# Running sums and maxima in a mixture-of-experts router: a chain of small additions, or one masked product and one reduction

## The chip, the core and the metric

The kernel runs on one core of one Trainium2 chip. The metric is device time in microseconds (us) of one execution; before the change the median of three runs is 1411.22 us (1411.13 to 1414.11). A profile is one execution recorded by the hardware profiler. Its times are counted from the start of its span, and all places in time below are such times.

## What is computed

A decoder layer over 16 sequences of 100 tokens (1600 tokens, width 512): self-attention, cross-attention over 361 context positions, and a feed-forward part with 8 experts, each part followed by a residual sum and a layer norm. The change touches the feed-forward part's routing:

```python
logits = jnp.einsum('bsd,de->bse', x, router_w) + router_b
topk_vals, topk_idx = jax.lax.top_k(logits, TOP_K)          # TOP_K = 2 of E = 8
topk_w = jax.nn.softmax(topk_vals, axis=-1)
full_w = jnp.sum(jax.nn.one_hot(topk_idx, E, dtype=x.dtype) * topk_w[..., None], axis=-2)
h = jnp.einsum('td,edf->etf', xf, expert_w) + expert_b[:, None, :]
combined = jnp.einsum('etf,te->tf', jax.nn.silu(h), full_w.reshape(-1, E))
out = jnp.einsum('bsd,df->bsf', combined, proj_w) + proj_b
y = x + out
return norm_w * (y / jnp.sqrt(jnp.mean(y * y, axis=-1, keepdims=True) + EPS))
```

## The kernel before

**Tiles.** The 1600 tokens are 13 tiles (`NT`) of 128 tokens, the last one of 64. Each token is sent to two experts. The kernel sorts the 3200 (token, expert) pairs into 32 slots (`NSL`) of 128 rows, each slot belonging to one expert, so that an expert product runs over 128 full rows. For each slot it gathers the rows of `x2d` by an indirect DMA on GpSimd's queue (`e_gather`, L1265), transposes them on TensorE (`e_turn`, tile `pte`, L1281), splits the transposed rows into a high and a low part (ScalarE writes the high part, L137, VectorE or GpSimd the low part, L140) and multiplies them by the expert's weights in three products (`e_product`, tile `ph`, L145 to L147, whose weights' address is read from the table `wat` by TensorE's sequencer, L1287). Every matmul of this kernel is such a triple over a high and a low part.

**Order.** Each engine runs its instructions in a fixed order, which a scheduler chose when the program was built; it may interleave the source's statements. An instruction that waits holds up everything behind it on its engine. POOL in the profile is GpSimd, DVE is VectorE, ACT is ScalarE, SP is the queue that issues most DMAs.

**Routing, in three steps.** `choose(a, b)` (L1041) takes the two best experts of the tokens in tiles a to b and counts, by two small matmuls (L1080), each token's rank within its expert; a third one (L1091) gives counts per tile. `settle(a, b)` (L1135) decides which slot each (tile, expert) opens. `slots(a, b, upto)` (L1231) turns this into lists of row indices for the slots a to b: small matmuls (L1239) of `named` (a token's number at its place in a slot, L1126) with `is_in` (the slot of a token, L1224), then the copies `idx`, `wat` and `bat` (L1247 to L1251), on which the gathers and the expert products wait.

This happens twice. The tiles 0 to 8 (`CUT` is 9) are settled while the last products of cross-attention's output projection still run (tile `acc`, L145 to L147, 128x512, four head products each of tiles 10, 11 and 12); that gives the slots 0 to 10 (`EARLY` is 11). The tiles 9 to 12 are settled while TensorE works on the early slots; that gives the slots 11 to 31.

**The code that changes.** In `settle` the helper `before_it` needs, for every tile, the number of slots opened by all earlier tiles. It keeps a running sum in `opened` (or `filled`), one VectorE addition of one element per tile:

```python
for t in range(a, b):
    nc.vector.tensor_tensor(
        till[:, t + 1 : t + 2], till[:, t : t + 1], here[:, t - a : t - a + 1], ALU.add)
```

(L1168). It runs for `opened` over 9 tiles and later 4, and for `filled` over 9. A third loop (L1207) keeps the running maximum `last`, 8 elements per tile, over 9 and later 4 tiles. `settle` then ends with `new` (L1211 to L1218), `tile_of` (L1223) and `is_in` (L1224), each twice from L1222 on.

**Around it.** While the first settle runs, VectorE also makes low parts `ot_l` of what the `acc` products read, and GpSimd makes low parts `ot_l` and `WL` (L140). `WL` belongs to expert weights, which arrive by DMA as `f_e` (L1320). The attention output arrives as `of` (L822).

Of the kernel before, what the change touches and what calls it, by code (L numbers as in the profile page):

```python
# [9 lines left out]
FP = mybir.dt.float32  # L10
FR = mybir.dt.float32r
AF = mybir.ActivationFunctionType
ALU = mybir.AluOpType
AX = mybir.AxisListType
# [13 lines left out]
NE = 8  # L28
# [34 lines left out]
def tile_decoder_layer(  # L63
# [28 lines left out]
    nc = tc.nc  # L92
# [3 lines left out]
    def pool(stack, name, bufs=1, **k):  # L96
        return stack.enter_context(
            tc.tile_pool(name=name, bufs=bufs, reuse_waits="tile", **k)
        )
# [115 lines left out]
    NT = len(TT)  # L215
# [56 lines left out]
    for k in range(KC):  # L272
# [8 lines left out]
        out=causal,  # L281
        in_=causal,
        compare_op=ALU.is_ge,
        fill=1.0e30,
        base=0,
        pattern=[[-1, S]],
        channel_multiplier=1,
# [526 lines left out]
    parts = [(t, g) for t in range(NT - TAIL) for g in range(NKV)]  # L814
# [94 lines left out]
    gw = pool(gs, "gate", side="right")  # L909
# [55 lines left out]
    I32, HF = mybir.dt.int32, mybir.dt.float16  # L965
    NSL = NE + (2 * T - NE) // 128
    CUT, EARLY = NT - 4, 11
# [3 lines left out]
    def iota(p, shape, pattern, base=0, mult=0, name=""):  # L971
# [17 lines left out]
        out=before,  # L989
        in_=before,  # L990
        compare_op=ALU.is_gt,
        fill=0.0,
        base=0,
        pattern=[[1, 128]],
        channel_multiplier=-1,
# [5 lines left out]
        out=lower,  # L1001
        in_=lower,
        compare_op=ALU.is_gt,
        fill=0.0,
        base=0,
        pattern=[[1, NE], [-1, NE]],
        channel_multiplier=0,
# [5 lines left out]
    cum = gw.tile([128, NT + 1, NE], HF, name="cum")  # L1013
    nc.vector.memset(cum[:, 0, :], 0.0)
    full = gw.tile([128, NE], FP, name="full")
    opened = gw.tile([128, NT + 1], FP, name="opened")
    nc.vector.memset(opened[:, 0:1], float(EARLY))
    filled = gw.tile([128, CUT + 1], FP, name="filled")
    nc.vector.memset(filled[:, 0:1], 0.0)
    last = gw.tile([128, NT + 1, NE], FP, name="last")  # L1020
    nc.vector.memset(last[:, 0, :], 0.0)
    rank = gw.tile([128, NT, NE], FP, name="rank")
    lo = gw.tile([128, 2, NT], FP, name="lo")
    tile_of = gw.tile([128, 2, NT], FP, name="tile_of")
# [4 lines left out]
    def by_128(dst, src, name):  # L1029

        i = gw.tile(list(dst.shape), I32, name=f"i_{name}")
        nc.vector.tensor_copy(i, src)
        nc.vector.tensor_scalar(i, i, 7, None, ALU.arith_shift_right)
        nc.vector.tensor_copy(dst, i)

    def table(name, shape, dt=FP):

        size = [128, CUT + 1, *shape[2:]]
        return gw.tile(size, dt, name=name, tag=name)[:, : shape[1]]
# [95 lines left out]
    def settle(a, b):  # L1135

        m = b - a
        sh = [128, m, NE]
        o2, o3 = 2 * NE + CUT * NE, (2 + CUT + m + 1) * NE
        count = gb[:, o2:o3].rearrange("p (b e) -> p b e", e=NE)  # L1140
        if a == 0:
            by_128(full, count[:, m, :], "full")

        up = table("up", [128, m + 1, NE])
        nc.vector.tensor_scalar(up, count, 127.0, None, ALU.add)
        had = table("had", [128, m + 1, NE])
        by_128(had, up, f"had_{a}")

        opn = table("opn", sh)
        nc.vector.tensor_tensor(opn, had[:, 1:, :], had[:, :m, :], ALU.subtract)  # L1150
        had = had[:, :m, :]
        sh4 = [128, m, NE, NE]

        def before_it(these, till, less, name):

            part = table("parts", sh4, HF)
            nc.vector.tensor_tensor(
                part,
                lower.unsqueeze(1).to_broadcast(sh4),
                these.unsqueeze(2).to_broadcast(sh4),  # L1160
                ALU.mult,
            )
            new = table(name, sh)
            nc.vector.tensor_reduce(new, part, AX.X, ALU.add)
            here = table("here", [128, m])
            nc.vector.tensor_reduce(here, these, AX.X, ALU.add)
            for t in range(a, b):
                nc.vector.tensor_tensor(  # L1168
                    till[:, t + 1 : t + 2],
                    till[:, t : t + 1],  # L1170
                    here[:, t - a : t - a + 1],
                    ALU.add,
                )
            nc.vector.scalar_tensor_tensor(
                new,
                new,
                float(less),
                till[:, a:b].unsqueeze(2).to_broadcast(sh),
                ALU.subtract,
                ALU.add,  # L1180
            )
            return new


        new = before_it(opn, opened, EARLY if a else 0, "new")
        if a == 0:
            fills = table("fills", sh)
            nc.vector.tensor_tensor(
                fills, had, full.unsqueeze(1).to_broadcast(sh), ALU.is_lt
            )  # L1190
            nc.vector.tensor_tensor(fills, fills, opn, ALU.mult)
            first = before_it(fills, filled, 0, "first")

            nc.vector.scalar_tensor_tensor(
                new, first, float(EARLY), new, ALU.min, ALU.subtract
            )

            nc.vector.scalar_tensor_tensor(
                fills, first, float(EARLY), fills, ALU.is_lt, ALU.mult
            )  # L1200
            nc.vector.tensor_tensor(first, first, new, ALU.add)
            nc.vector.tensor_tensor(first, first, fills, ALU.mult)
            nc.vector.tensor_tensor(new, first, new, ALU.subtract)

        nc.vector.tensor_tensor(opn, opn, new, ALU.mult)
        for t in range(a, b):
            nc.vector.tensor_tensor(  # L1207
                last[:, t + 1, :], last[:, t, :], opn[:, t - a, :], ALU.max
            )
        old = last[:, a:b, :]  # L1210
        nc.vector.tensor_tensor(new, new, old, ALU.subtract)  # L1211

        past = table("past", sh)
        nc.vector.scalar_tensor_tensor(
            past, had, 128.0, rank[:, a:b, :], ALU.mult, ALU.is_le
        )
        nc.vector.tensor_tensor(new, new, past, ALU.mult)
        nc.vector.tensor_tensor(new, new, old, ALU.add)  # L1218
        sh3 = [128, m, NSL]
        for j in range(2):  # L1220
            mine = table("chose", sh)
            nc.vector.tensor_tensor(mine, one[:, j, a:b, :], new, ALU.mult)  # L1222
            nc.vector.tensor_reduce(tile_of[:, j, a:b], mine, AX.X, ALU.add)  # L1223
            nc.vector.tensor_tensor(  # L1224
                is_in[:, j, a:b, :],
                seq[:, :NSL].unsqueeze(1).to_broadcast(sh3),
                tile_of[:, j, a:b].unsqueeze(2).to_broadcast(sh3),
                ALU.is_equal,
            )
# [98 lines left out]
    for i in range(HEAD * NKV, len(parts)):  # L1328
        t, g = parts[i]
# [29 lines left out]
        if (t, g) == (CUT, 3):  # L1359
            settle(0, CUT)  # L1360
            slots(0, EARLY, CUT)
# [29 lines left out]
    with tc.high_priority(offset=URGENT):  # L1391
        choose(CUT + 1, NT)
        settle(CUT, NT)
        slots(EARLY, NSL, NT)
# [412 lines left out]
```

## Time and profile before

| what | us |
|---|---|
| median of the runs | 1411.22 |
| the profiled execution, whole | 1423.84 |
| its span | 1422.1 |
| first `settle` to the end of its `is_in`, on VectorE | 1178.8 to 1212.0 |
| first lookup matmuls (L1239), TensorE | 1211.16 to 1213.2 |
| gathers of the slots 0 to 3 issued, GpSimd | 1213.90 to 1219.1 |
| second `settle` to its last `is_in` | 1252.8 to 1261.9 |
| second lookups end, TensorE | 1266.3 |
| first gather of the second list issued | 1267.17 |
| TensorE starts on the first gathered rows of the second list | 1273.74 |

The profiled execution took 12.6 us longer than the median of the runs, so differences are taken within the trace and then set against the median. In the timelines a row reads: start, duration, engine, line, operation, output<-inputs, size, count, and in square brackets how long the engine sat idle before it and what ended that. A row with a count (x7) covers that many instructions in a row. The granted clock (PEclk) is TensorE's clock as a share of full speed.

### The profile page before, as it was taken

Reading aid. Unit: us, or ns where it says so; the run is one execution under the profiler, and the core shown is the slowest. Engines: PE = TensorE matmul, PEld = TensorE weight load, DVE = VectorE, ACT = ScalarE, POOL = GpSimd, SP = SyncE. Lnnn points to the kernel's source line nnn. Section 1 sums busy time; section 2 is a strip of 40 time slices with the busy share of each in tenths; the row PEclk is TensorE's granted clock in tenths of the full one; section 3 lists DMA queues with packets and bytes.
Section 4 is the critical chain, followed back from the end, with each engine's and each line's share of the span. In section 5 each row is a group of like instructions: output and inputs, shape, how many; then the busy total and the mean of one; then the engine's idle time right before and its main releaser. Section 6 shows DMA issues by size and latency. Waiting matters only on the chain.

```text
span 1422.1 us, 25158 instructions
## 1 busy us (share of the span) xinstructions
PE 1338.8 (94%) x7952; PEld 1109.5 (78%) x7952; DVE 939.8 (66%) x2960; ACT 756.9 (53%) x1899; POOL 708.8 (50%) x837
## 2 busy tenths in 40 slices
PE   8999989999999999999999999999999897899895
PEld 6888868888878887888888788878887675677773
DVE  5776577776467777767777667767653658654577
ACT  4666653444445666666565666656563233233356
POOL 6877663344245555555555545545454345431530
PEclk9999989999999999999999999999999999799997
DMA  5221254545442222233233213232536555667773
GB/s 158 72 93 51 73 158 115 130 91 111 101 93 77 53 60 69 70 77 76 69 70 82 70 43 70 70 70 54 132 84 198 170 167 164 189 207 232 247 254 125
DMA packets 197872, 159.79 MB, mean 112 GB/s; under 512 B 133322, under 2 KB 152878, under 8 KB 197742
## 3 DMA queue, kind: packets, MB, share of 16 engines
q1 hardware_dynamic: 187904, 137.83, 36.3%
q0 software_dynamic: 4576, 14.95, 3.5%
q10 hardware_dynamic: 5262, 5.41, 1.3%
q8 instruction: 65, 1.06, 0.3%
q14 instruction: 65, 0.53, 0.1%
HBM read 107.16 MB, written 50.99 MB: 111 GB/s over the span
## 4 chain that ended last, share of the span: by engine, by line
PE 69%; DVE 13%; DMA 8%; ACT 4%; issue 3%; POOL 1%; SPq 1%; ACTq 0%; DVEq 0%; POOLq 0%
PE pq L145 4%; PE pq L147 4%; PE pq L146 4%; PE pv L145 4%; PE pv L146 4%; PE pv L147 4%; PE ptp L767 3%; PE pk L145 3%; PE pk L147 3%; PE pk L146 3%; PE s L145 3%; PE s L147 3%; PE s L146 3%; PE av L146 2%; PE av L145 2%
## 5 line engine op out<-in xcount | busy, mean ns | idle before, releaser
L759 POOL TENSOR_SCALAR p<-p,sums 100x361 f32<-100x361 f32 x256 | 146.5, 577 | 100.2 <-DVE sums L758 89.2
L746 DVE CUSTOM_DVE_ANT_0 p<-s,nmask 100x361 f32<-100x361 f32 x256 | 132.9, 527 | 64.4 <-PE s L147 56.0
L757 ACT ACTIVATE p<-p,nm 100x361 f32<-100x361 f32 x256 | 153.2, 601 | 40.1 <-DVE nm L746 37.0
L140 DVE TENSOR_TENSOR pT_l<-ptp,pT_h 128x400 fp32r<-128x400 f32 (+1 forms) x192 | 107.4, 567 | 57.3 <-ACT pT_h L137 56.7
L145 PE MATMUL pq<-WH 128*128 128x512 f32 (+2 forms) x272 | 107.2, 394 | 5.7 <-DVE WH L139 5.7
L767 PE MATMUL ptp<-ident,p 100*128 100x100 f32 (+1 forms) x768 | 107.5, 252 | 0.0
L137 ACT CAST pT_h<-ptp 128x400 fp32r<-128x400 f32 (+1 forms) x192 | 91.2, 486 | 29.6 <-PE ptp L767 29.1
L767 PEld LDWEIGHTS ptp<-ident,p 100*128 100x128 f32 (+1 forms) x768 | 95.6, 152 | 13.4 <-POOL p L759 2.3
L140 POOL TENSOR_TENSOR cT_l<-cf,cT_h 128x512 fp32r<-128x512 f32 (+1 forms) x48 | 54.3, 1133 | 101.9 <-ACT cT_h L137 100.0
L146 PE MATMUL pq<-WL,WH 128*128 128x512 f32 (+2 forms) x272 | 104.6, 385 | 0.0
L147 PE MATMUL pq<-WH,WL 128*128 128x512 f32 (+2 forms) x272 | 104.5, 384 | 0.0
L147 PE MATMUL acc<-WH,ot_l 128*128 128x512 f32 (+1 forms) x208 | 85.9, 414 | 7.4 <-DVE ot_l L140 5.6
L145 PE MATMUL acc<-WH,ot_h 128*128 128x512 f32 (+1 forms) x208 | 85.8, 413 | 4.9 <-ACT ot_h L137 4.9
L145 PE MATMUL s<-kT_h,WH 128*100 128x362 f32 x256 | 88.2, 355 | 1.7 <-ACT kT_h L137 1.7
L145 PE MATMUL av<-pT_h,WH 128*128 128x400 f32 (+1 forms) x192 | 77.3, 402 | 11.5 <-ACT pT_h L137 11.2
L147 PE MATMUL s<-kT_h,WL 128*100 128x362 f32 x256 | 84.5, 330 | 0.0
L146 PE MATMUL acc<-WL,ot_h 128*128 128x512 f32 (+1 forms) x208 | 84.3, 405 | 0.0
L146 PE MATMUL s<-kT_l,WH 128*100 128x362 f32 x256 | 83.9, 328 | 0.0
L614 POOL TENSOR_TENSOR qs<-qs,r_q 128x512 f32<-128x512 f32 (+1 forms) x52 | 54.0, 1068 | 59.3 <-DVE r_q L169 48.9
L140 POOL TENSOR_TENSOR WL<-qf,WH 128x400 fp32r<-128x400 f32 x64 | 67.3, 1052 | 30.1 <-ACT WH L137 26.7
L145 PE MATMUL pv<-WH,cT_h 128*128 128x512 f32 (+1 forms) x192 | 79.6, 414 | 0.9 <-DVE WL L140 0.9
L145 PE MATMUL pk<-WH,cT_h 128*128 128x512 f32 (+1 forms) x192 | 77.6, 404 | 0.2
(336 smaller groups left out, 4007.0 us busy)
## 6 DMA issues: line engine op xcount, KB each, us to landing
qf<-qd SPq DMA_DIRECT2D x64, 200.0 KB
of<-od SPq DMA_DIRECT2D x48, 256.0 KB
cf<-in_ctxT SPq DMA_DIRECT2D x16, 722.0 KB
eb<-in_expert_b SPq DMA_DIRECT2D x32, 256.0 KB
ysd<-h SPq DMA_DIRECT2D x32, 256.0 KB
f_e<-in_expert_w SPq DMA_DIRECT2D x30, 256.0 KB
f_wq<-in_Wq SPq DMA_DIRECT2D x16, 256.0 KB
f_wo<-in_Wo SPq DMA_DIRECT2D x16, 256.0 KB
```

The costliest lines, as they stand in the source:

```text
L137: ins = nc.scalar.copy(dst.h, src)
L140: low.tensor_tensor(dst.l, src, dst.h.bitcast(FP), ALU.subtract)
L145: nc.tensor.matmul(out, a.h, b.h, start=start, stop=False)
L146: nc.tensor.matmul(out, a.h, b.l, start=False, stop=False)
L147: nc.tensor.matmul(out, a.l, b.h, start=False, stop=stop)
L614: nc.gpsimd.tensor_tensor(qr[:, hs, :], qr[:, hs, :], rs[:n, hs].unsqueeze(2).to_broadcast([n, GR, HD2]), ALU.mult,)
L746: nc.vector.tensor_tensor_reduce(out=p, in0=sc[:, :SE], in1=nmask, scale=1.0, scalar=BIG, op0=ALU.add, op1=ALU.min, accum_out=nm,)
L757: nc.scalar.activation(p, p, AF.Exp, bias=nm, scale=-1.0, accum_out=sh)
L759: nc.gpsimd.tensor_scalar(p, p, sh, 1.0, ALU.mult, ALU.mult)
L767: nc.tensor.transpose(pt[:n, h, :], probs[h][:, c0 : c0 + n], ident[:S, :S])
```

## The change

The three loops go. A constant table `earlier` of 13 x 13 elements is made once on GpSimd (a memset and an affine select): it is 1 where the second tile number is below the first. The sum over earlier tiles is then one VectorE product of `earlier` with the per-tile values and one reduction; the maximum over earlier tiles is a product of 9 x 8 x 9 elements (later 4 x 8 x 13) and one reduction by max. The three tables that held the running values lose their start elements and the memsets of these.

```diff
+    earlier = gw.tile([128, NT, NT], FP, name="earlier")
+    nc.gpsimd.memset(earlier, 1.0)
+    nc.gpsimd.affine_select(
+        out=earlier, in_=earlier, compare_op=ALU.is_gt, fill=0.0, base=0,
+        pattern=[[1, NT], [-1, NT]], channel_multiplier=0,
+    )
...
-            here = table("here", [128, m])
-            nc.vector.tensor_reduce(here, these, AX.X, ALU.add)
-            for t in range(a, b):
-                nc.vector.tensor_tensor(
-                    till[:, t + 1 : t + 2],
-                    till[:, t : t + 1],
-                    here[:, t - a : t - a + 1],
-                    ALU.add,
-                )
+            nc.vector.tensor_reduce(here[:, a:b], these, AX.X, ALU.add)
+            tri = parts_of([128, 1, m, b])[:, 0]
+            nc.vector.tensor_tensor(
+                tri,
+                earlier[:, a:b, :b],
+                here[:, :b].unsqueeze(1).to_broadcast([128, m, b]),
+                ALU.mult,
+            )
+            till = table("till", [128, m])
+            nc.vector.tensor_reduce(till, tri, AX.X, ALU.add)
...
-        nc.vector.tensor_tensor(opn, opn, new, ALU.mult)
-        for t in range(a, b):
-            nc.vector.tensor_tensor(
-                last[:, t + 1, :], last[:, t, :], opn[:, t - a, :], ALU.max
-            )
-        old = last[:, a:b, :]
+        nc.vector.tensor_tensor(places[:, a:b, :], opn, new, ALU.mult)
+        sh5 = [128, m, NE, b]
+        prior = parts_of(sh5)
+        nc.vector.tensor_tensor(
+            prior,
+            places[:, :b, :].rearrange("p t e -> p e t").unsqueeze(1).to_broadcast(sh5),
+            earlier[:, a:b, :b].unsqueeze(2).to_broadcast(sh5),
+            ALU.mult,
+        )
+        old = table("old", sh)
+        nc.vector.tensor_reduce(old, prior, AX.X, ALU.max)
```

`parts_of` gives one shared scratch tile `parts` of 648 half-precision elements, used by all these products and by the older product with `lower` (L1157). Since the scheduler orders the whole program anew, the change also moves instructions that it doesn't touch. Set side by side, the two builds have TensorE's stream equal up to the last `acc` products, and then the following moves:

- The first lookups (L1239) stand two `acc` matmuls earlier.
- The count matmuls of the last `choose` (L1080, L1091) stand inside the transposes of slot 5, not of slot 6; the first 18 lookups of the second list stand ahead of the products of slot 5, not 6; and its other 34 stand inside the transposes of slot 9, ahead of the products of slot 8, not inside those of slot 10.
- The transposes of slot 11, the first of the second list, stand ahead of the products of slot 10, not behind them.
- On VectorE the rest of the last `choose` (all but one of its additions `cum`, L1075) stands ahead of the bias sum `h` of slot 2 (L1306), not behind it, and the settle after it is one slot earlier among the `h` and `xsT_l` instructions.
- On GpSimd the six `named` of the last tiles (L1126) stand ahead of the gather of slot 10, not behind it.

More of the change, by code (lines that the diff above doesn't have):

```diff
@@ L1015, in tile_decoder_layer @@
     full = gw.tile([128, NE], FP, name="full")
[L1016 to L1021, printed above, removed]
+    earlier = gw.tile([128, NT, NT], FP, name="earlier")
+    nc.gpsimd.memset(earlier, 1.0)
+    nc.gpsimd.affine_select(
+        out=earlier,
+        in_=earlier,
+        compare_op=ALU.is_gt,
+        fill=0.0,
+        base=0,
+        pattern=[[1, NT], [-1, NT]],
+        channel_multiplier=0,
+    )
+    opened = gw.tile([128, NT], FP, name="opened")
+    filled = gw.tile([128, CUT], FP, name="filled")
+    places = gw.tile([128, NT, NE], FP, name="places")
     rank = gw.tile([128, NT, NE], FP, name="rank")
@@ L1034, in by_128, with parts_of @@
         nc.vector.tensor_copy(dst, i)
+    parts_ = CUT * NE * (NE + 1)
+    def parts_of(shape):
+        f = gw.tile([128, parts_], HF, name="parts", tag="parts")
+        a, b, c = shape[1:]
+        f = f[:, : a * b * c]
+        return f.rearrange("p (a b c) -> p a b c", a=a, b=b, c=c)
     def table(name, shape, dt=FP):
@@ L1152, in settle, with before_it @@
         sh4 = [128, m, NE, NE]
-        def before_it(these, till, less, name):
-            part = table("parts", sh4, HF)
+        def before_it(these, here, less, name):
+            part = parts_of(sh4)
             nc.vector.tensor_tensor(
@@ L1177, in before_it @@
                 float(less),
-                till[:, a:b].unsqueeze(2).to_broadcast(sh),
+                till.unsqueeze(2).to_broadcast(sh),
                 ALU.subtract,
@@ L1182, in before_it @@
             return new
-        new = before_it(opn, opened, EARLY if a else 0, "new")
+        new = before_it(opn, opened, 0 if a else -EARLY, "new")
         if a == 0:
```

## The prediction

> **What bounds the kernel now.** I read the page's first two parts, then TensorE's waits late in the span, then the timelines around them.
>
> ```profile
> PE 1338.8 (94%) x7952; PEld 1109.5 (78%) x7952; DVE 939.8 (66%) x2960; ACT 756.9 (53%) x1899; POOL 708.8 (50%) x837
> ...
> PEclk9999989999999999999999999999999999799997
> ```
>
> TensorE is busy 94% of the span, so the kernel is bound by its products; only its holes can be gained. Two holes lie where routing happens. The first, in the timelines of TensorE, VectorE and POOL (GpSimd):
>
> ```profile
> 1206.02 0.39 PE L146 MATMUL acc<-WL,ot_h 128*128 128x512 f32 x1
> 1211.16 0.17 PE L1239 MATMUL gb<-is_in,named 128*128 128x11 f16 x1 [4.75 <-DVE is_in L1224]
> 1212.06 0.60 PE L1239 MATMUL gb<-is_in,named 128*128 128x11 f16 x17 [0.73 <-DVE is_in L1224]
> ...
> 1213.60 0.63 PE L146 MATMUL acc<-WL,ot_h 128*64 128x512 f32 x1
> ```
>
> ```profile
> 1191.52 4.57 DVE L1168 TENSOR_TENSOR opened<-opened,here 128x1 f32<-128x1 f32 x7
> ...
> 1201.88 0.77 DVE L1207 TENSOR_TENSOR last<-last,opn 128x8 f32<-128x8 f32 x4
> ...
> 1203.21 6.20 DVE L1207 TENSOR_TENSOR last<-last,opn 128x8 f32<-128x8 f32 x5
> ```
>
> ```profile
> 1202.91 4.03 POOL L140 TENSOR_TENSOR WL<-f_e,WH 128x512 fp32r<-128x512 f32 x3 [3.48 <-ACT WH L137]
> ```
>
> TensorE idles 4.75 + 0.73 = 5.5 us for `is_in`, the last step of the first settle. Afterwards its clock is down: by windows the granted clock is 0.64 in 1212 to 1220, matmuls start 0.43 us apart instead of 0.23, and the eleven up to 1217.6 lose 11 x 0.20 = 2.2 us more. `is_in` is late because of the additions the change removes. Alone, four `last` steps take 0.77 us. Beside GpSimd's L140 five take 6.20 us, one per GpSimd instruction (its 4.03 us for three): each VectorE addition waits for one to end.
>
> The second hole, in GpSimd's and TensorE's timelines:
>
> ```profile
> 1267.17 1.03 POOL L1265 DMA_INDIRECT xs<-x2d,idx  x1 [7.55 <-DVE bat L1251]
> ```
>
> ```profile
> 1273.74 0.63 PE L1281 MATMUL pte<-ident,xs 128*128 128x128 f32 x4 [1.75 <-DMA xs<-x2d,idx]
> ...
> 1276.38 0.76 PE L145 MATMUL ph<-WH,xsT_h 128*128 x1 [1.00 <-issue]
> ```
>
> The second list's first gather takes 1273.74 - 1267.17 = 6.57 us, and TensorE had only the products of slots 9 and 10 to cover it. It idles 1.75 us, has further gaps of 0.38, 1.00 and 0.34 us, and runs at clock 0.59 in 1276 to 1284 (twelve products at 0.43: 2.4 us lost). Later waits follow TensorE's own output, so what is gained here I carry to the end.
>
> **Part 1: the first settle.** Removed: 27 additions, 9 + 9 of one element and 9 of eight. Summing intervals from the first of each group to what follows it: 0.84 + 0.11 + 4.49 + 0.49 + 2.63 + 0.72 + 6.12 = 15.4 us, of which 27 x 0.18 = 4.9 are work and the rest stalls. Added: two products and two reductions of 81 elements (128x72 steps take 0.26 us when each waits for the last: 1.0), one product of 648 and its reduction. Their near row:
>
> ```profile
> L1157 DVE TENSOR_TENSOR parts<-lower,opn 128x576 f16<-128x576 f32 x1 | 0.8, 753 | 0.0
> ...
> L1157 DVE TENSOR_TENSOR parts<-lower,opn 128x256 f16<-128x256 f32 x1 | 0.4, 415 | 0.0
> ```
>
> (753 - 415)/320 = 1.06 ns per element, so 648 take 0.83 us, the reduction (754 ns at 576) the same. Added 2.7 us.
>
> Here a rule speaks against the change: the Trainium skill, SBUF — State Buffer (Door 1: The DMA port swizzle), says memory is read in lines of 16 bytes and steps across lines cost extra. The new product reads `places` in steps of 8 floats, 32 bytes. No row has such a step. The row gives 0.83 us; doubled by the rule, 1.7 us. I take 0.83 and keep 1.7 for the range; neither reaches TensorE, as follows.
>
> I walk the new VectorE order through GpSimd's old times. 1188.9: reduction `filled`. `ot_l` waits for GpSimd till 1189.8 and ends about 1190.15, as now, so TensorE's wait there (3.43 us, till 1190.20) stays. `till`, `new`, the second `parts` and its reduction: 1192.4. Then three two-input steps, each held by one of the three `WL` up to 1195.4. Three more, and `ot_l` of tile 11 at 1196.5 (was 1197.6). The long product and reduction to 1199; two `WL`/`ot_l` stalls to 1200.3; five steps to 1201.4; `ot_l` of tile 10, whose transfer SP issues when the former `ot_l` frees its buffer, to about 1201.8; `is_in` about 1203.1, or 1206.2 if it meets the `WL` run from 1202.9. TensorE, with the lookups two matmuls earlier, comes there at 1205.8. So 5.5 us of idling falls to 0 to 0.5, and without the idle window the 2.2 us of slow clock go too.
>
> What is late next: `ot_l` of tile 12. Its high part is ready on ScalarE only at 1208.2, then GpSimd's `WL` runs to 1209.4; so it ends at 1209.75 and TensorE waits about 1.5 us. It still finishes `acc` at about 1214.4 instead of 1220.4. But VectorE's `idx` copy stands behind that `ot_l`: 1210.5 instead of 1213.5. The gathers gain 3.0 us, not 6. Slot 0's products began at 1223.42 behind slot 1's transposes (1222.50), so I expect them at 1220.4, plus half of the short waits behind them (0.43 to 0.60 us each): **gain 3.5 us**. Bounds: 1.5 if the new hole ahead of the gathered rows draws a slow-clock window, 6 if the gathers land faster.
>
> **Part 2: the second settle.** The arithmetic is even: 8 additions at 0.2 = 1.7 us removed; 52- and 416-element steps added, about 0.2 + 0.2 + 0.6 + 0.6 = 1.6 us. What counts is the order. The rest of `choose`, now held behind `h` of slot 2 (VectorE idles 3.34 us at 1244.82 with it in the queue), goes ahead of it, and counts, settle and lookups move up one product, 3.2 us. On the old time scale TensorE comes to the last 34 lookups at 1261.9; `is_in` should stand at 1259.2, behind `h` of slot 6: 2.7 us of slack. Lookups end near 1263.1, `idx` behind `xsT_l` of slot 9 at 1263.9, first gather at 1264.3, landed at 1270.8. TensorE has slot 8's products, a transpose and slot 9's products to 1263.1 + 2.75 + 0.45 + 2.75 = 1269.05: a hole of 1.75 us stays, but slot 10's products come after it and nothing is slowed. Slot 11's products end at 1270.8 + 2 x (0.45 + 2.75) + 0.9 for reads of `wat` = 1278.1 instead of 1282.3: **gain 4.2 us**.
>
> The moved `named` (4.81 us for six) stand ahead of slot 10's gather: `lo` at 1250.9, `named` done at 1255.7, gather landed by 1262.4, needed at 1265.7. Covered by 3.3 us. Do these `named` stall VectorE?
>
> ```profile
> 1254.81 4.81 POOL L1126 TENSOR_SCALAR named<-seq,lo,token 128x128 f16<-128x128 f32 x6 [1.58 <-DVE lo L1114]
> ```
>
> ```profile
> 1256.95 0.77 DVE L1168 TENSOR_TENSOR opened<-opened,here 128x1 f32<-128x1 f32 x3
> ```
>
> The Trainium skill, SBUF — State Buffer (Who interferes with whom), says a VectorE instruction with two SBUF inputs is shut out while GpSimd runs any instruction that reads SBUF. By that, six waits of up to 0.8 us: 4.8 us, 2.1 beyond the slack, and the gain is 2.1 instead of 4.2. The rows disagree: under six `named` three such additions take 0.77 us, no stall. I go by the rows.
>
> **Part 3: the rest.** GpSimd gains a memset and an affine select of 128x169 (128x64 takes 0.14 and 0.28 us: about 1.0 together). They lie at 1086, ahead of an idle stretch of 1.32 us and one of 1.08 us; without that cover `seq` and `token` come 1 us late, with VectorE idle 2.80 us behind them. Three memsets of 0.06 us go. SP's reads of `bat` move with `idx`. In the tail ScalarE takes one square before the high part of tile 11: 0.7 us late, hidden behind the products of tile 10: 0.
>
> **Sum.** 3.5 + 4.2 = 7.7 us: 1423.84 becomes 1416.1 in a profiled execution, and 1411.22 becomes **1403.5**. The profile is 12.6 us above the median; I assume the holes are alike.
>
> **Rivals.**
> - *Forecast*, both holes shrink, gains of 4.5 to 11 us (1400 to 1407): 0.57.
> - *Both close*, gathers land sooner and slow-clock windows vanish: 6 + 4.2 + 1.75 + up to 2 = 12 to 14 us, 1398. For: the holes cost 7.7 and about 6 us now. Against: `idx` behind `ot_l`. 0.13.
> - *Hidden anyway*: the first gain is eaten waiting for gathered rows and a slow window (1.5), the second by stalls or a gather (1): about 1409. For: the gap from 1214.9 to 1220 is new. 0.22.
> - *Slower*: the moved lookups. TensorE runs in order; if `named` or `is_in` is late there it stands still, where before it had another product. Each us beyond the slack of 2.7 costs one. With Part 1's 3.5 kept, the sign turns at 2.7 + 4.2 + 3.5 = 10.4 us of lateness, and 13 give 1414. Against: nothing in the rows stalls so long. 0.08.
>
> About 0.2% (2.8 us: 1408.4 to 1414.0) can be told from no change. Faster: 0.57 + 0.13 + 0.1 of the third case = 0.80; same: 0.12 of the third; slower 0.08. The range, 1396.5 to 1410, leaves out the slower case and the ends.
>
> **What would show it.** After: no idle before the first lookups and full clock behind them; no VectorE step of 1.2 us more than about six times in the settle; first gathers 3 us earlier against the same start; the long product at 0.83 us; first wait for `xs` of the second list ahead of slot 10's products, under 2.5 us. I am wrong if TensorE idles at the 34 lookups, or if the first gain doesn't outlast slot 0.

## The result, and the profile after

The changed kernel takes 1403.6 us (median of 7 runs, 1401.56 to 1407.8) where the kernel before took 1411.72 beside it (7 runs, 1408.32 to 1417.3): a ratio of 0.9947, 95% interval 0.9932 to 0.9963, or 8.1 us. The profiled execution has a span of 1401.2 us, close to its median; the one before had 1422.1, some 12 above. So of the 20.9 us between the two traces a good part is not the change: 7.2 us lie ahead of the count matmuls of the first settle (at 1178.46 before, at 1171.29 after), where no instruction was altered. From here on times are counted from that matmul, and traces are used for where time goes, the runs for how much.

The page of the changed kernel, busy time of the engines and granted clock in 40 slices:

```profile
PE 1334.0 (95%) x7952; PEld 1107.1 (79%) x7952; DVE 938.7 (67%) x2932; ACT 757.9 (54%) x1899; POOL 712.5 (51%) x839
...
PEclk9999999999999999999999999999999999899997
```

VectorE has 28 instructions fewer and is busy for 1.1 us less. TensorE has as many as before and is busy for 4.8 us less: fewer of them ran at the low clock (mean granted clock 0.979, before 0.973). What the change gives is in its holes.

TensorE's timeline ahead of the first lookups, in the changed kernel:

```profile
1191.69 0.50 PE L147 MATMUL acc<-WH,ot_l 128*128 128x512 f32 x1 [2.68 <-DVE ot_l L140]
...
1201.25 0.61 PE L1262 MATMUL gb<-is_in,named 128*128 128x11 f16 x18
1201.78 0.59 PE L1262 MATMUL gb<-is_in,opens 128*1 128x11 f16 x18
1202.31 0.50 PE L145 MATMUL acc<-WH,ot_h 128*128 128x512 f32 x1
```

No bracket stands behind the lookups: the 5.5 us of waiting for `is_in` are gone. TensorE still waits for `ot_l`, 3.6 us in all where it was 3.4, but at another place: the wait of 3.43 us that the prediction left standing is 0.92 us here, and the 2.68 us are for the `ot_l` of tile 11. The second hole, in GpSimd's and in TensorE's timeline:

```profile
1252.62 0.94 POOL L1288 DMA_INDIRECT xs<-x2d,idx  x1 [6.42 <-DVE bat L1274]
```

```profile
1257.76 0.60 PE L1304 MATMUL pte<-ident,xs 128*128 128x128 f32 x4
...
1259.87 0.50 PE L147 MATMUL ph<-WH,xsT_l 128*128 x1 [0.69 <-DVE xsT_l L140]
```

The first gather of the second list is issued at 81.3 us after the counts (88.7 before), and the transposes of slot 11 find their rows there 5.1 us later, without any wait. Before, the same gather took 6.57 us and TensorE stood still for 1.75.

VectorE's timeline of the first settle, where the additions were:

```profile
1184.49 1.85 DVE L1174 TENSOR_TENSOR parts<-lower,fills 128x576 f16<-128x576 f32 x1
...
1189.82 1.21 DVE L1219 TENSOR_TENSOR first<-first,new 128x72 f32<-128x72 f32 x1
1190.96 0.68 DVE L140 TENSOR_TENSOR ot_l<-of,ot_h 128x512 fp32r<-128x512 f32 x1
...
1192.35 1.36 DVE L1226 TENSOR_TENSOR parts<-places,earlier 128x648 f16<-128x648 f32 x1
```

Steps that take 0.75 and 0.23 us alone still take 1.85 and 1.21 beside GpSimd's L140, and they put off the `ot_l` of tile 11 which TensorE waits for. The product of 648 elements takes 1.36 us, with GpSimd idle from 1190.94 to 1197.27.

### The profile page after: what moved, and what is told of

Its sections match the earlier page's. It is cut to its first block, busy times and chain, and to the rows that moved or that the text cites. A ratio compares the mean times of both kernels' runs of the same rounds, so it can differ in the third digit from the quotient of the medians.

```text
span 1401.2 us, 25131 instructions
## 1 busy us (share of the span) xinstructions
PE 1334.0 (95%) x7952; PEld 1107.1 (79%) x7952; DVE 938.7 (67%) x2932; ACT 757.9 (54%) x1899; POOL 712.5 (51%) x839
## 5 line engine op out<-in xcount | busy, mean ns | idle before, releaser
L140 DVE TENSOR_TENSOR pT_l<-ptp,pT_h 128x400 fp32r<-128x400 f32 (+1 forms) x192 | 107.4, 567 | 56.2 <-ACT pT_h L137 55.5
L140 POOL TENSOR_TENSOR cT_l<-cf,cT_h 128x512 fp32r<-128x512 f32 (+1 forms) x48 | 54.3, 1133 | 104.6 <-ACT cT_h L137 102.6
L140 POOL TENSOR_TENSOR WL<-qf,WH 128x400 fp32r<-128x400 f32 x64 | 67.3, 1053 | 30.0 <-ACT WH L137 26.2
L146 PE MATMUL pv<-WL,cT_h 128*128 128x512 f32 (+1 forms) x192 | 78.1, 407 | 0.0
```

What stands on the lines that cost most here:

```text
L140: low.tensor_tensor(dst.l, src, dst.h.bitcast(FP), ALU.subtract)
L146: nc.tensor.matmul(out, a.h, b.l, start=False, stop=False)
```

## Experiments

Two theories were set against each other. **A**: both parts of the change count, the arithmetic in the first settle and the new order in the second. **B**: the order that the scheduler (the expectations call it the planner) lays out is all. The table has every kernel that ran. "is_in", "idx" and "slot 5" are the end of the first list's `is_in`, the start of its `idx` copy and of the first transpose of slot 5, in us after the counts; "5 to 13" is from there to the first transpose of slot 13 (behind the products of slot 11), which holds the second hole. These come from one trace each; runs of one kernel spread over 5 to 15 us, so the ratio (to the kernel before on the same chip) decides on the whole. The chips differ in level (the kernel before has medians of 1411.7 to 1428.9 us on them), so where an expectation names a time, its ratio is what to compare.

| kernel | ratio, 95% interval | is_in | idx | slot 5 | 5 to 13 |
|---|---|---|---|---|---|
| before, first trace | 1 | 33.5 | 35.0 | 69.5 | 34.4 |
| before again | 0.9997 (0.9979 to 1.0015) | 35.1 | 36.5 | 70.4 | 34.6 |
| changed, first trace | 0.9947 (0.9932 to 0.9963) | 27.6 | 32.1 | 65.4 | 28.8 |
| changed again | 0.9945 (0.9928 to 0.9962) | 28.6 | 30.5 | 62.6 | 28.2 |
| old sums, changed tables | 0.9946 (0.9929 to 0.9964) | 30.1 | 34.5 | 65.0 | 28.7 |
| old first settle | 0.9948 (0.9931 to 0.9966) | 31.4 | 33.4 | 66.5 | 28.8 |
| old second settle | 0.9940 (0.9918 to 0.9962) | 27.8 | 29.8 | 63.1 | 30.1 |
| before with one name | 0.9949 (0.9932 to 0.9967) | 30.2 | 32.1 | 65.5 | 28.1 |
| maxima alone | 0.9980 (0.9968 to 0.9992) | 32.7 | 34.1 | 67.5 | 31.5 |
| `places` by expert | 0.9924 (0.9897 to 0.9950) | 28.5 | 30.4 | 63.0 | 29.4 |
| running values in PSUM | 0.9960 (0.9944 to 0.9976) | 30.9 | 32.4 | 64.9 | 33.2 |
| mask and `new` in PSUM | 0.9906 (0.9885 to 0.9927) | 26.2 | 29.4 | 61.1 | 27.9 |
| the same, `places` by expert | 0.9902 (0.9880 to 0.9924) | 24.7 | 29.1 | 59.6 | 28.6 |
| that one again | 0.9915 (0.9896 to 0.9933) | 24.9 | 29.3 | 61.4 | 27.6 |

### The kernel before, once more

No edit.

> The kernel before once more, unchanged: its ratio must hold 1.000, and it shows how far one program's trace differs from execution to execution. Each theory: the first trace of it was some 12 us above the median of its runs, with 7.2 us of the difference to the changed kernel ahead of the first settle; a second trace should lie nearer to 1411, and from the `rank` copy that starts the first settle to the end of the span it should take 236 to 244 us (first trace 243.4; changed kernel 229.7). TensorE's two holes (4.75 + 0.73 us ahead of the first lookups, 1.75 us ahead of slot 10's products) should be there again, within 1 us each.

Measured: 0.9997. TensorE's waits at the two places, in its second trace:

```profile
1221.02 0.17 PE L1239 MATMUL gb<-is_in,named 128*128 128x11 f16 x1 [0.85 <-DVE is_in L1224]
1222.98 0.57 PE L1239 MATMUL gb<-is_in,named 128*128 128x11 f16 x17 [1.80 <-DVE is_in L1224]
```

```profile
1283.98 0.63 PE L1281 MATMUL pte<-ident,xs 128*128 128x128 f32 x4 [1.74 <-DMA xs<-x2d,idx]
1285.23 0.63 PE L1281 MATMUL pte<-ident,xs 128*128 128x128 f32 x4 [0.62 <-DMA xs<-x2d,idx]
```

The second hole came back within 0.01 us. The first is 2.65 us here, not 5.5, though `is_in` is later (35.1): TensorE had waited 4.8 us for `ot_l` ahead of it, not 3.4. The wait in front of the lookups is therefore a poor measure of the first hole; the times of `idx` and slot 5 are steadier. From the counts to the end of TensorE's last matmul this trace has 231.3 us and the first 231.2; from the `rank` copy to the end of the span it has 242.6, within the 236 to 244 expected.

### Old arithmetic in the changed tables, in one settle or both

The changed kernel's tables and scratch tile stay; the sums and maxima are taken tile by tile again. Both settles:

```diff
-            tri = parts_of([128, 1, m, b])[:, 0]
-            nc.vector.tensor_tensor(tri, earlier[:, a:b, :b], ..., ALU.mult)
-            till = table("till", [128, m])
-            nc.vector.tensor_reduce(till, tri, AX.X, ALU.add)
+            for t in range(a, b):
+                nc.vector.tensor_tensor(
+                    run[:, t + 1 : t + 2], run[:, t : t + 1], here[:, t : t + 1], ALU.add)
+            till = run[:, a:b]
...
-        nc.vector.tensor_reduce(old, prior, AX.X, ALU.max)
+        for t in range(a, b):
+            nc.vector.tensor_tensor(
+                last[:, t + 1, :], last[:, t, :], places[:, t, :], ALU.max)
+        old = last[:, a:b, :]
```

> The changed kernel's tables and its order of instructions in the second settle (counts and lookups one product earlier), but with the sums and maxima taken tile by tile as before in both settles. Theory A (both parts of the change count: the order of the second settle, and the fewer VectorE steps of the first): the second hole closes but the first is back, so 4 to 5 us of the 8.1 are kept: 1406 to 1409, ratio to the kernel before 0.996 to 0.998. Rival B (the order is all): 1403 to 1404, ratio 0.995. Rival C (the steps of the first settle are all): 1411, ratio 1.000. In the trace by A: about 5 us of TensorE idle ahead of the first lookups as before, one-element additions at about 0.6 us each, and no wait of over 1 us at the first transposes of the second list.

Only the first settle, or only the second, by an `if` on `a` around the same edit:

> The changed kernel with the first settle alone taken tile by tile as before; the second settle by products and reductions. By Theory A the same as with both settles tile by tile, since the second settle's arithmetic is about even: 1406 to 1409, ratio 0.996 to 0.998, the idle time of about 5 us ahead of the first lookups back. Rival B: 1403 to 1404. Rival C: 1411.

> The changed kernel with the second settle alone taken tile by tile (eight additions of 0.2 us, and one reduction for each of the three running values to start from); the first settle by products and reductions. The order of instructions is the changed kernel's. By Theory A and by Rival B: as the changed kernel within 1 us, 1403 to 1405, ratio 0.994 to 0.996, no wait at the first transposes of the second list. By Rival C also, since the first settle is the new one. If it is slower by over 3 us, the products and reductions of the second settle are worth that themselves, which none of the three says.

Measured: 0.9946, 0.9948 and 0.9940. All 35 additions and maxima are back in the first of them, and the whole gain stays; theory A's 0.996 to 0.998 is missed, and its 5 us of idling ahead of the first lookups didn't come back either: TensorE waits for `is_in` by 0 and 1.53 us in the first two. So the gain doesn't need the new arithmetic. In the table "5 to 13" is 28.7 with old sums, as with new ones, and slot 5 comes at 65.0 us instead of 69.5 to 70.4. (Not by way of `idx` in this trace, which is only 0.5 us earlier than in the first of before; but the 22 `acc` matmuls behind the lookups run at full clock and take 4.9 us, where they took 7.3 at a granted clock of 0.68.) The last of the three waited 0.60 us for the rows of slot 11, where no wait was expected. What these kernels share with the change is that the sums per tile, `here`, no longer lie in one buffer for both uses in the first settle.

### The kernel before with one name changed

```diff
-            here = table("here", [128, m])
+            here = table("here_" + name, [128, m])
```

> The kernel before with one word changed: the small table that holds the sums of each tile, `here`, gets a buffer for each of its two uses in the first settle instead of one for both. No product, no mask, no reduction is added; all additions and maxima are taken tile by tile as before. The planner then lays out the same orders as for the changed kernel: the two chains of additions interleave, the first lookups stand ahead of the last products of tile 11, and the counts and lookups of the second settle come one product earlier. Theory B (the planner's order is all of the gain, and the shared `here` was what held it): as fast as the changed kernel within 0.2%, ratio 0.993 to 0.996, no wait for `xs` of the second list. Theory A (the arithmetic of the first settle counts as well): 0.996 to 0.998. Rival D (the separate mask or the separate `places` are needed): 1.000.

Measured: 0.9949, the interval of the change itself. VectorE's timeline in the first settle of this kernel:

```profile
1190.57 0.14 DVE L1168 TENSOR_TENSOR opened<-opened,here_new 128x1 f32<-128x1 f32 x1
1190.63 0.15 DVE L1168 TENSOR_TENSOR filled<-filled,here_first 128x1 f32<-128x1 f32 x1
1190.74 1.21 DVE L1168 TENSOR_TENSOR opened<-opened,here_new 128x1 f32<-128x1 f32 x1
1191.87 0.15 DVE L1168 TENSOR_TENSOR filled<-filled,here_first 128x1 f32<-128x1 f32 x1
...
1199.12 1.78 DVE L1207 TENSOR_TENSOR last<-last,opn 128x8 f32<-128x8 f32 x9
```

With one `here`, the reduction that fills it for `filled` had to wait until the ninth addition to `opened` had read it, so the chains ran one after the other. With two they alternate, and each held step serves both. The maxima then come early enough to fall between two runs of GpSimd (idle from 1198.5 to 1201.9): nine take 1.78 us, where in the first trace of before five of them met a run of five GpSimd instructions and took 6.20. The scheduler's order for this kernel also has the counts and lookups of the second settle one product earlier, as in the change; what in the scheduler leads from the one to the other isn't shown. TensorE's timeline at the two places, the first lookups and the transposes of slot 11:

```profile
1207.64 0.57 PE L1239 MATMUL gb<-is_in,named 128*128 128x11 f16 x17 [1.95 <-DVE is_in L1224]
...
1263.98 0.60 PE L1281 MATMUL pte<-ident,xs 128*128 128x128 f32 x4
```

The second hole is gone. At the first, TensorE still waits 1.95 us for `is_in`, whose last steps met GpSimd's next run (from 1201.90); nevertheless slot 5 comes as early as in the first trace of the change. In the ratio, one word does what the change does.

### The counterpart: the changed maxima, with one shared `here`

The changed kernel, its sums by loop over `table("here", [128, m])` as before; the maxima stay a product and a reduction.

> The counterpart: the changed kernel with its maxima by product and reduction, but the sums tile by tile over one shared `here`, as before. The planner lays out the order of before: lookups behind the first products of tile 11, counts behind the products of slot 4, the second list's lookups behind slot 8. Nine maxima of eight elements (0.77 us for four without stalls, 6.20 for five with) are gone from the first settle and four from the second. Theory B: as before, ratio 0.998 to 1.001, the wait of 1.7 us for `xs` of the second list is back. Theory A: the first hole shrinks, since a third of the steps with two inputs are gone: ratio 0.996 to 0.998, with the second hole back.

Measured: 0.9980, interval 0.9968 to 0.9992: some 3 us of 1424, on the border between the two theories. TensorE's timeline at the two places:

```profile
1211.38 0.17 PE L1267 MATMUL gb<-is_in,named 128*128 128x11 f16 x1 [1.67 <-DVE is_in L1252]
1212.96 0.58 PE L1267 MATMUL gb<-is_in,named 128*128 128x11 f16 x17 [1.41 <-DVE is_in L1252]
...
1273.20 0.63 PE L1309 MATMUL pte<-ident,xs 128*128 128x128 f32 x4 [0.50 <-DMA xs<-x2d,idx]
```

In the old order the arithmetic is worth something: the interval leaves out 1, and slot 5 comes 2.0 to 2.9 us sooner. The second hole is smaller too, though the order is old: the gather landed within 4.9 us in this trace, with all but one of the 34 lookups two matmuls into the products of slot 9. The next run shows what the arithmetic is worth in the new order.

### The change again, beside the kernel with one name

> The changed kernel once more, beside the one with one word changed: ratio 0.993 to 0.996 by every theory, and a second trace of it. Theory A: faster than the kernel with one word by 3 to 4 us. Theory B: within 2 us of it. Ahead of the first lookups TensorE should idle less than 1 us, and at the first transposes of the second list not at all; the 128x648 product should take 1.36 us again.

Measured: 0.9945 against 0.9949 with one name; medians 1415.92 and 1416.43 on the same chip. The difference of 0.5 us can't be told from nothing, and up to some 3 us either way can't be excluded. `is_in` does come sooner with the products (27.6 and 28.6 against 30.2). In the first trace of the change little came of that: `is_in` ended at 1198.9, but TensorE, held up by the `ot_l` of tile 11, came to the lookups only at 1201.25, and `idx` starts at 32.1, as with one name. In its second trace TensorE waits 0.74 us for `is_in`, doesn't wait for the rows of slot 11, and has slot 5 at 62.6, 2.9 us sooner than with one name; the long product takes 1.47 us.

### The step of 32 bytes

```diff
-    places = gw.tile([128, NT, NE], FP, name="places")
+    places = gw.tile([128, NE, NT], FP, name="places")
```

and the step that writes it and the product that reads it follow the new layout.

> The changed kernel with the table `places` kept with the tiles innermost, so that the 648-element product reads neighbouring floats; nothing else differs, and the order on every engine is the same. If the step of 32 bytes is what made that product dear, it takes 0.8 to 0.9 us instead of 1.36 (the 416-element one 0.6 instead of 0.99); if it is something else (the mask's own broadcast, the size), it stays at 1.3. The whole time is that of the changed kernel within 1 us in either case, since TensorE doesn't wait for that step.

Measured: the two products (416 and 648 elements), by tile in this kernel, and below it in the one of the next section that has its mask in PSUM as well, so that they have one SBUF input. The columns are count, shortest/mean/longest in ns, and first to last start:

```profile
L1228 DVE TENSOR_TENSOR parts<-places,earlier x2: 593/1176/1760, 1199.5 to 1249.8; 128x648 f16<-128x648 f32 x1, 128x416 f16<-128x416 f32 x1
```

```profile
L1233 DVE TENSOR_TENSOR parts<-places,gb x2: 589/710/830, 1197.6 to 1245.1; 128x648 f16<-128x648 f32 x1, 128x416 f16<-128x416 f32 x1
```

The shorter one falls from 0.99 to 0.59 us; the longer one met GpSimd's L140 in the first kernel (1.76), and takes 0.83 in the second. With the step it took 1.36, 1.47 and 1.49 us in three traces with both inputs in SBUF (1.84 in a fourth, beside L140), and 1.44 with the mask in PSUM. So the step of 32 bytes, not the mask, makes it dear: 2.1 to 2.4 ns per element instead of 1.3 to 1.4. The ratio of this kernel, 0.9924, has a wide interval that overlaps the changed kernel's; whether the layout shortens the whole is open, and the last section speaks against it.

### Is it two SBUF inputs that are held?

The old arithmetic in the changed tables, but the running values lie in PSUM:

```diff
-    run_o = gw.tile([128, NT + 1], FP, name="run_o")
+    run_o = gb[:, 200 : 200 + NT + 1]
```

and `run_f` and `last` in the same way.

> The kernel with the old arithmetic in the changed kernel's tables, but with the running sums and maxima in PSUM, so that each of the 27 additions of the first settle reads one operand from SBUF and one from PSUM. It tests the step of the prediction that an addition with two SBUF inputs waits for the GpSimd instruction beside it to end. If so, none of the 27 takes over 0.3 us beside L140's 1.3-us instructions, and they fill about 27 x 0.2 = 5.4 us in all where they took 15.4 in the first trace of before. If one SBUF input is enough to be held, some still take 1.2 us. The planner lays out another order for this kernel: the first lookups come two matmuls later than before, and the second list's all together behind slot 8, as late as before. By Theory B (the order decides) the second hole is back and the time is 0.997 to 1.000 of before; by Theory A 0.995 to 0.997.

Measured: VectorE and GpSimd in this kernel, then in the second trace of before:

```profile
1192.02 1.36 DVE L1194 TENSOR_TENSOR gb<-gb,opened 128x1 f32<-128x1 f32 x7
```

```profile
1191.88 3.76 POOL L140 TENSOR_TENSOR WL<-f_e,WH 128x512 fp32r<-128x512 f32 x3 [1.51 <-ACT WH L137]
```

```profile
1202.10 3.96 DVE L1168 TENSOR_TENSOR opened<-opened,here 128x1 f32<-128x1 f32 x7
```

```profile
1201.44 3.82 POOL L140 TENSOR_TENSOR WL<-f_e,WH 128x512 fp32r<-128x512 f32 x3
```

Both times seven additions start beside the same run of three GpSimd instructions. With two inputs from SBUF they take 3.96 us and end 0.8 us behind the last `WL`; with one from PSUM they take 0.19 us each, as if GpSimd weren't there, and are done while the second `WL` runs. Here the result goes to PSUM too, so the output could be the reason instead; the next section's long product, with one input from PSUM and its result in SBUF, speaks against that (0.83 us in its last kernel, begun while a `WL` ran). This is the mechanism that the prediction assumed, now shown. The rest of the settle kept its stalls (`is_in` at 30.9).

The scheduler gave this kernel the late order in the second settle, "5 to 13" is 33.2, and the ratio 0.9960: some 70% of the change's gain, with slot 5 at 64.9. That is below Theory B's 0.997 to 1.000 (the interval just reaches 0.997), so the first settle counts as well. That the vanished stalls of the additions brought this is not shown: with the same additions and tables in SBUF slot 5 came at 65.0, and what the two kernels share is again a `here` for each use.

### The mask and `new` in PSUM

The changed kernel with this edit, and with `places` by expert as above:

```diff
+    early_ps = gb[:, 200 : 200 + NT * NT].rearrange("p (a b) -> p a b", b=NT)
+    nc.vector.tensor_copy(early_ps, earlier)
...
-            new = table(name, sh)
+            if name == "new":
+                new = gb[:, 370 : 370 + m * NE].rearrange("p (t e) -> p t e", e=NE)
+            else:
+                new = table(name, sh)
...
-                earlier[:, a:b, :b],
+                early_ps[:, a:b, :b],
```

> The changed kernel with `places` by expert, and with the mask `earlier` and the table `new` in PSUM, so that the products and most steps of the first settle have one SBUF input at most. If the stalls come from two SBUF inputs, the first settle's steps of 0.9 to 1.9 us fall to 0.2 to 0.8, the long product takes 0.8 us whatever GpSimd does, and `ot_l` of tile 11, behind them in VectorE's queue, ends 1 to 3 us earlier, which TensorE waited for by 2.1 to 2.7 us. By Theory B nothing further is to be had from arithmetic: ratio 0.992 to 0.996, as the changed kernel. If that wait was worth its length: 0.991 to 0.993, below every kernel so far.

Then without the edit of `places`, and the whole once more:

> The changed kernel with the mask `earlier` and the table `new` in PSUM, but `places` laid out as in the change, with the step of 32 bytes. It tells which of the two edits of the fastest kernel so far (0.990) is worth something. If it is PSUM (fewer held steps ahead of the first lookups): 0.989 to 0.992, with the long product at 1.3 to 1.5 us and off the path. If it is the layout of `places`: 0.993 to 0.996, as the changed kernel.

> The fastest kernel so far once more, beside the one with the mask in PSUM alone: 0.988 to 0.993 if its first result holds, with the first counts to slot 5's transposes again in 59 to 61 us (62.8 to 65.6 in the changed kernel, 69.5 to 70.4 before). If that result came by chance of the clock, 0.993 to 0.996.

Measured: 0.9902, 0.9906 and 0.9915. All three are below the changed kernel, whose two results are 0.9947 and 0.9945; it is the PSUM edit, with the order that the scheduler made for it, that does it, since the one with the step of 32 bytes is as fast. TensorE's timeline of that one at the first lookups:

```profile
1208.67 0.18 PE L1267 MATMUL gb<-is_in,named 128*128 128x11 f16 x1
1209.11 0.57 PE L1267 MATMUL gb<-is_in,named 128*128 128x11 f16 x17 [0.26 <-DVE is_in L1252]
```

`is_in` ends at 24.7 to 26.2 us instead of 27.6 to 28.6, `idx` starts at 29.1 to 29.4 instead of 30.5 to 32.1, and slot 5 at 59.6 to 61.4 instead of 62.6 to 65.4; "5 to 13" is the change's. (The repeat's 61.4 lies just above the 59 to 61 expected.) Theory B's "nothing further from arithmetic" fell here: the edit was worth another 0.4%, some 5 us. This is the fastest version found, 11 to 13 us below the kernel before in the medians.

That the gain comes from steps no longer held is argued, and only in part shown. For it: TensorE's order up to slot 5 is the changed kernel's, and `is_in` comes sooner. Against it: steps that still read twice from SBUF stay held (the second product with `lower` takes 1.13 to 1.16 us, 0.74 alone), and the whole of the gain isn't found in the traces: from the counts to the end of TensorE's last matmul the three kernels have 215.9, 218.4 and 218.5 us, the changed kernel 218.6 and 218.2. The scheduler also put all of the second list's lookups into one place for these kernels; what that alone is worth isn't known.

## Why the prediction was right or wrong

The time was right, 1403.5 against 1403.6, and both places were the right ones. The cause was wrong in half, so part of the closeness is luck: the old additions keep most or all of it once `here` has a buffer for each use, which the prediction never looks at and the change brought along.

**"`is_in` is late because of the additions the change removes" is the step that failed.** The additions are held by GpSimd as it said (0.19 us each with an operand in PSUM, 3.96 us for seven without). But they need not go: with all of them kept and one name changed, `is_in` comes 3.3 us sooner than in the first trace of before (5.9 in that of the change), and slot 5 at 65.5 us after the counts, against 69.5 to 70.4 before and 65.4 and 62.6 in the change. The shared `here` had put the two chains end to end, and in the first trace that pushed the maxima into GpSimd's next run. The walk through the new VectorE order priced the removed steps and didn't ask what else had kept them in line.

**First gain, 3.5 us.** The gathers of the first list start at 32.9 us instead of 35.4 in the two first traces, 2.5 us sooner where 3.0 were forecast, and slot 5 comes 4.1 us sooner. The size was right. That TensorE doesn't wait at the first lookups and its clock is full behind them was right as well (0.74 us of waiting in the second trace). But a slow window stands ahead of them: the matmuls are 0.43 us apart from 1192.36 to 1195.34, behind the 2.68 us of waiting for the `ot_l` of tile 11, as one stood before behind the wait of 3.43 us. The walk put this `ot_l` at 1196.5, 18.0 us after the counts; it ended 20.4 after.

**The long product at 0.83 us: wrong, 1.36.** The rule on 16-byte lines (the Trainium skill, SBUF — State Buffer, Door 1: The DMA port swizzle) was nearer than the row of a contiguous product: the page says that crossing lines costs, but gives no factor, and the doubling to 1.7 was the prediction's own estimate. With the layout contiguous the row's 0.83 was met exactly. As forecast, TensorE didn't wait for it in the first trace of the change, where it came to the lookups 2.3 us after `is_in` was done.

**Second gain, 4.2 us, "what counts is the order".** Right, and too small: "5 to 13" shrank by 5.6 us. The mis-sized term is the gather's 6.57 us. Taken over from before, it left a hole of 1.75 us; the gather landed within 5.1 us and no hole was left. Why it lands sooner isn't known. And the order was taken as coming with the new arithmetic; the one name is enough for it.

**`named` beside VectorE.** The prediction went by the rows against the rule of the same page of the Trainium skill (SBUF — State Buffer, Who interferes with whom), which would have cost 2.1 us of the gain. The rows held: in the change, VectorE steps with two SBUF inputs take 0.32, 0.19 and 0.99 us under the six `named` from 1240.00 to 1245.01, none of them longer by the 0.8 us of a `named`. The clearest pair is the 416-element product in the layout by expert: 0.59 us under `named` with both inputs in SBUF, and 0.59 with the mask in PSUM. GpSimd's L140, with two inputs, shuts VectorE out; `named`, with one tensor input, did not do so in any trace here.

**The sum.** In the runs 8.1 us against 7.7. Between the first traces the two places give 4.1 + 5.6 = 9.7 us, and from the counts to the end of TensorE's last matmul 12.7; what lies between that and the runs' 8.1 is within the spread of single executions, and isn't explained further.

**The rivals.** The slower case needed TensorE to stand at the second list's lookups; it didn't, in any kernel. "Both close" was right about the second hole and wrong about the first. What "Hidden anyway" feared held for the arithmetic alone: on top of the new order its gain can't be told from nothing.

## What to carry to other kernels

A scratch table that two independent chains share ties them together end to end, and a scheduler then lays the rest of the program around that; before chains are rewritten, give each use its own buffer and look at the order again. This case has one scheduler and one such table. Where a change moves instructions as well as replacing them, run the moves without the replacement: here a one-word edit had all of the gain that could be measured. And where VectorE works beside GpSimd, look at what its steps read as well as at how many they are: two tables moved to PSUM, with the order that came of it, were worth another 0.4%, where replacing 35 small steps was worth nothing that could be told on top of the new order.

## What the runs showed of the hardware

- Seven dependent one-element additions on VectorE took 3.96 us beside three GpSimd subtractions of 128x512 with both operands in SBUF, and 1.36 us in the same place, with one operand and the result in PSUM.
- Conversions and integer shifts with a single SBUF input can be held as well: in the first settle of the kernel with mask and `new` in PSUM, VectorE's L1044, L1045, L1131 and L1132 (8, 8, 6 and 6 integers) took 1.28, 1.15, 1.23 and 1.23 us beside GpSimd's run, and their neighbours with 80 elements (L1043, L1044, L1045) 0.19, right behind a step that had just been let in.
- Six GpSimd `named` (128x128, one tensor input, 0.8 us each) didn't hold a VectorE product of 416 elements with both inputs in SBUF: 0.59 us, as with one of them in PSUM.
- A product with one operand read in steps of 32 bytes took 2.1 to 2.4 ns per element, with neighbouring floats 1.3 to 1.4.
